# A graph attention layer on one core: four weight sums of the last head as DMA additions, with new orders for the last two heads

## The chip, the cores and the metric

The kernel runs on one core of one Trainium2 chip. The metric is the device time of one execution in microseconds (us). Engines are named as in the profile: PE is TensorE's matmul, PEld its weight load, DVE is VectorE, ACT is ScalarE, POOL is GpSimd, SP is SyncE, which here only issues DMAs. Each engine runs its own instructions strictly in the order in which they were written, and waits where an instruction needs the result of another engine or of a DMA.

## The reference

512 nodes with 768 features, 16,896 directed edges, eight attention heads in layer one and one in layer two; then a residual and a layer norm.

```python
def gat_layer(x, W, a_s, a_d, b, edge_index, concat):
    h = (x @ W).reshape(n, H, C)
    alpha_s = jnp.einsum('nhc,hc->nh', h, a_s)
    alpha_d = jnp.einsum('nhc,hc->nh', h, a_d)
    e = jax.nn.leaky_relu(alpha_s[src] + alpha_d[dst], NEG_SLOPE)
    m = jax.ops.segment_max(e, dst, num_segments=n)
    e = jnp.exp(e - m[dst])
    denom = jax.ops.segment_sum(e, dst, num_segments=n)
    alpha = e / (denom[dst] + EPS)
    out = jax.ops.segment_sum(h[src] * alpha[:, :, None], dst, num_segments=n)
    return out.reshape(n, H * C) + b          # here concat=True

h = gat_layer(x, W1, a_src1, a_dst1, b1, edge_list, concat=True)   # 8 heads of 768
h = jax.nn.elu(h)
out = gat_layer(h, W2, a_src2, a_dst2, b2, edge_list, concat=True) # W2: 6144 x 768
result = _layernorm(x + out, axis=-1)
```

## The kernel before

Edges are counted into a dense 512 x 512 matrix, so that each head is: a projection with W1 (512 x 768 by 768 x 768), a dense softmax over the logits, a product of the softmax with the projected features, an ELU, and a product with the head's 768 rows of W2, whose results are added up in the tile `h2` over all heads. After head 7 (the last) the second layer's softmax and its product with `h2` follow, then the layer norm and the output.

**Fewer products, more sums.** Each of these matrix products is done with fewer multiplications than the plain one. The softmax product of a head cuts both sides into 2 x 2 blocks and takes seven products, P1 to P7 (`mixed`, lines 960 to 1040; matmuls at L972). The W2 product cuts W2's 768 x 768 into 3 x 3 blocks of 256 x 256 and takes fifteen products, P0 to P14 (`second_thirds`, matmuls at L550; DVE empties a bank into `h2` at L558). Its left operands are sums of blocks of the ELU's output `gT` (`g_thirds`, DVE at L584 and L587). Its right operands are W2's blocks or sums of them, and these sums are made in two ways by `load_thirds`. Four of them are done while the block is loaded: SP loads one block, and POOL then issues a DMA that adds another block from HBM to it (`join`, L187). Eight more, called `w.P0`, `w.P1`, `w.P2`, `w.P3`, `w.P4`, `w.P6`, `w.P7`, `w.P10`, are additions of 128 x 512 elements by DVE (L200). `w.P0` adds block P12 to block P0, `w.P4` adds P13 to P4, `w.P1` and `w.P7` add P6 to P1 and P7; each writes over its own operand.

**Order.** Nothing is scheduled by the program itself. Strings of names fix the order in which the operations are written, and with it each engine's order: HEAD and SECOND for the heads, NEXT for the projection of the head after, END for head 7 and the whole second layer. HEAD's third string is used for head 6 alone. In these strings P10 to P72 are the seven softmax products for the three column chunks 0 to 2, `x`, `y`, `N`, `B`, `F` with a chunk's number are DVE's steps behind them (L990 for `x` and `y`, L1007, L1014, L1024), `b`, `f`, `n`, `nn`, `u`, `w` ACT's steps, `g.P..` the left sums, `m.P..` the W2 products, `e.P..` their emptying. `src`, `dst` (L420) and in END `ls`, `ld` (L1258) are row products of DVE for the logits; `rank`, `leak` (DVE) and `lift`, `out`/`part`, `in` (ACT) belong to the softmax; `l0` to `l3` and `r0` to `r3` are the sums of the next softmax product's operands.

**Around the change.** `loads` (one name in HEAD) issues all loads and joins of W2's rows of head 7 into the tiles `w2r` and `w2t`, during head 6. `vectors` loads the two vectors of the second layer's logits into `w1t` (L1192) at the end of head 6. Then x is loaded again by SP, and POOL adds the bias b2 to it by four DMAs of 384 KB (L1254). `rows0` and `rows1` (L1267) are the matmuls that make the second layer's logits; `spread` (L1289) and `own` (L1295) hand them on.

Of the kernel before, what the change touches and what calls it, by code (L numbers as in the profile page):

```python
# [37 lines left out]
def gat_pass(  # L38
# [119 lines left out]
    def load_thirds(slot, m, apart):  # L158

        def of(rows, k):  # L160
            return rows[k:k + HK + 1:HK] if apart else rows[2 * k:2 * k + 2]

        chunks = list(range(DC))

        def third(k, n):
# [16 lines left out]

        def load(o, k, n):
            return lambda: nc.sync.dma_start(o, part(k, n))

        def join(o, k, n):
            return lambda: nc.gpsimd.dma_start(o, part(k, n), accum_op=add)  # L187

        def row(k):
            return lambda: nc.sync.dma_start(rows_[:, k, :], m[k * P:(k + 1) * P, :])  # L190

        loads = {f"r{k}": row(k) for k in range(DC)}
        loads.update(P1=join(third(1, 1), 1, 2), P14=join(third(2, 1), 0, 1), p13=load(P13, 0, 2), P13=join(P13, 2, 2),
                     p12=load(P12, 0, 0), P12=join(P12, 1, 0), p11=load(P11, 0, 1), P11=join(P11, 1, 1))
        raw = {(k, n): third(k, n) for k in range(3) for n in range(3)}
        B_ = dict(P8=raw[0, 2], P9=raw[0, 0], P5=raw[0, 1], P13=P13, P12=P12, P14=raw[2, 1], P4=raw[2, 0], P0=raw[1, 2],
                  P3=raw[2, 2], P7=raw[1, 0], P1=raw[1, 1], P6=square(two, 0), P2=square(two, 1), P11=P11, P10=square(four, 1))

        def op(o, a, b, how):
            return lambda: nc.vector.tensor_tensor(B_[o], B_[a], B_[b], op=how)  # L200
# [552 lines left out]
    if not general:  # L753
# [85 lines left out]
    else:  # L839
# [252 lines left out]
    ops = softmax(q, 0)  # L1092
# [32 lines left out]
    def hold():  # L1125
# [25 lines left out]
        P61 P70 u1 w0 w.P6 x0 P71 P40 b0 vadd ls2 P30 w.P10 y0 w1 B0 P51 P62 w.P0 P41 u2 x1 w.P2 b1 P72 w2 ls3 w.P4 ld2 B1  # L1151
        P31 P42 f0 y1 P52 f1 F0 m.P2 x2 b2 ld1 F1 P32 B2 g.P9 g.P12 y2 m.P9 e.P2 w.P1 f2 m.P12 ld3 F2 g.P7 rows0 e.P9 g.P1
        w.P3 rows1 row2 e.P12 g.P13 m.P1 g.P6 g.P11 spread e.P1 m.P0 own m.P13 2lift1 w.P7 2lift2 2lift0 2leak1 g.P10 e.P0
        2rank1 m.P10 e.P13 2lift3 2leak0 2rank0 m.P4 2part1 e.P10 2leak2 2part0 2rank2 m.P11 e.P4 g.P8 2leak3 m.P6 seed g.P3
        m.P8 2rank3 g.P14 e.P6 2den0 2den2 2part2 2in1 m.P14 e.P11 e.P8 g.P5 e.P14 2den3 2part3 m.P3 2in2 m.P7 e.P3 2in0
        2den1 m.P5 e.P7 2in3 root c0 e.P5 f.P1.0 a0 f.P1.1 f.fork0 a2 a1 c1 f.P2.0 c2 f.fork1 y11.0 f.P6.0 sq0 xu0 a3 c3
        f.P5.0 f.P7.0 f.P6.1 xw0 f.P4.0 y22.0 xu1 sq2 y21.0 bn2 f.P3.0 f.P7.1 y12.0 bn4 f.P5.1 all2 all0 xw1 inv0 inv2 whole2
        f.P4.1 y22.1 sq3 whole0 f.P2.1 y21.1 bn3 all3 f.P3.1 y11.1 inv3 bn1 right3 left3 y12.1 bn5 all1 hint inv1 left1
        right1"""
# [305 lines left out]
```

## Time and profile before

| | |
|---|---|
| three runs | 614.26, 615.30 and 615.68 us; median 615.3 |
| the profiled execution's own time | 615.11 us |
| its span in the profile | 613.3 us |
| TensorE's granted clock | 0.997 |
| head 6, softmax product up to its first W2 product | about 492 to 511 us |
| head 6, W2 products | about 511 to 537 us |
| head 7, softmax product | about 537 to 559 us |
| head 7, W2 products | about 556 to 587 us |
| second layer's product, layer norm, output | about 587 to 613 us |

The span runs from the first to the last recorded instruction; the profiled execution took 1.8 us more than it. Times below are microseconds from the span's start. A row of the timeline gives the start, the length, the engine, the line, the operation, what is written from what with the shape, the number of merged instructions, and in brackets the idle time before it with what ended it. Instructions of DVE that follow each other overlap a little: one that lasts 0.68 us lets the next start after 0.60.

### The profile page before, as it was taken

The page shows a single profiled execution, that of the slowest core. Times are in us where ns is not written, and L with a number is a line of the kernel's source. Part 1 is how long each engine was busy: PE and PEld are TensorE (multiplying, and loading weights), DVE is VectorE, ACT ScalarE, POOL GpSimd, SP SyncE. Part 2 cuts the span into 40 slices and gives each one's busy share as a digit, 9 for nine tenths or more (in the row PEclk, how much of TensorE's full clock was granted, in tenths as well). Part 3 has the DMA queues.
Part 4 walks back from the last instruction along what each step waited for, and adds up shares of the span by engine and source line. Part 5 has one row for each costly group of instructions (what it writes and reads, how often), then busy time and mean ns, then how long its engine had stood idle before and what let it go on. Part 6 is the DMA issues. An engine that isn't in the chain of part 4 may idle for free.

```text
span 613.3 us, 8350 instructions
## 1 busy us (share of the span) xinstructions
PE 601.6 (98%) x2809; PEld 492.0 (80%) x2809; DVE 518.8 (85%) x1029; ACT 307.0 (50%) x570; POOL 94.2 (15%) x139
## 2 busy tenths in 40 slices
PE   8999999999999999999999999999999999999994
PEld 5665685788888888888888888888888888877862
DVE  7979968779997789778897789968896789889975
ACT  3128776624745176433736066442746056744753
POOL 1210103040301302021300303022300303020000
PEclk9999999999999999999999999999999999999998
DMA  8983898794947959394956949296965949282212
GB/s 284 324 175 81 246 266 211 210 293 80 345 68 247 198 192 228 57 342 74 335 95 205 238 132 281 45 322 108 311 126 157 265 108 241 41 234 39 45 25 107
DMA packets 96399, 113.19 MB, mean 185 GB/s; under 512 B 42918, under 2 KB 77406, under 8 KB 95454
## 3 DMA queue, kind: packets, MB, share of 16 engines
q1 hardware_dynamic: 75374, 89.26, 46.1%
q0 software_dynamic: 20544, 22.75, 23.5%
q10 hardware_dynamic: 432, 0.59, 0.3%
q8 instruction: 24, 0.39, 0.2%
q14 instruction: 25, 0.20, 0.1%
HBM read 99.05 MB, written 2.90 MB: 166 GB/s over the span
## 4 chain that ended last, share of the span: by engine, by line
PE 91%; DVE 5%; DMA 3%; issue 1%; ACT 0%; SPq 0%; DVEq 0%; ACTq 0%
PE mm L550 23%; PE mm L470 18%; PE mm L972 14%; PE mm L411 11%; PE tr L470 4%; PE bc L470 4%; PE tr L972 3%; PE bc L972 3%; PE tr L550 3%; PE bc L550 3%; PE mm L1331 2%; DMA hs<-in_x_dram 2%; PE bc L781 1%; DVE scr L1258 1%; DMA w1t<-in_L_gnn_a_dst_dram 1%; PE mm L658 1%
## 5 line engine op out<-in xcount | busy, mean ns | idle before, releaser
L558 DVE TENSOR_TENSOR h<-h,mm 128x512 f32<-128x512 f32 x80 | 54.5, 681 | 9.3 <-PE mm L550 8.6
L476 ACT ACTIVATE hs<-mm 128x512 f32<-128x512 f32 x26 | 15.5, 598 | 80.6 <-PE mm L470 79.9
L187 POOL DMA_DIRECT2D w2t<-in_L_gnn_W_dram x21 | 28.3, 1665 | 165.7 <-DVE h L558 56.2
L478 DVE TENSOR_TENSOR hs<-hs,mm 128x512 f32<-128x512 f32 x38 | 26.1, 687 | 27.0 <-PE mm L470 19.9
L972 PE MATMUL mm<-PT,hs 128*128 128x256 f32 x196 | 47.8, 380 | 0.7 <-DVE gT L1007 0.7
L550 PE MATMUL mm<-w1r,gT 128*128 128x256 f32 x192 | 44.1, 379 | 0.0
L901 ACT ACTIVATE q<-q,rden 128x512 f32<-128x512 f32 x28 | 20.2, 720 | 46.1 <-DVE rden L885 45.8
L972 PEld LDWEIGHTS mm<-PT,hs 128*128 128x128 f32 x196 | 36.8, 190 | 6.4 <-ACT u L983 1.3
L909 ACT COPY PT<-zr 128x1024 uint16<-128x1024 uint16 x35 | 40.3, 1158 | 1.9 <-DMA zr<-pS 1.8
L550 PEld LDWEIGHTS mm<-w1r,gT 128*128 128x128 f32 x192 | 36.4, 190 | 5.1 <-DVE h L558 0.2
L187 POOL DMA_DIRECT2D w2r<-in_L_gnn_W_dram x14 | 18.3, 1310 | 140.6 <-DVE gT L1024 57.7
L698 ACT ACTIVATE q<-q,nmax 128x512 f32<-128x512 f32 x36 | 26.0, 723 | 25.3 <-DVE nmax L695 25.3
L470 PE MATMUL mm<-w2r,gT 128*128 128x256 f32 x144 | 33.7, 379 | 0.0
L420 DVE SCALAR_TENSOR_TENSOR scr<-hs,a_s 128x768 bf16<-128x768 f32 x32 | 30.6, 955 | 0.7
L420 DVE SCALAR_TENSOR_TENSOR scr<-hs,a_d 128x768 bf16<-128x768 f32 x32 | 30.4, 951 | 0.3
L470 PEld LDWEIGHTS mm<-w2r,gT 128*128 128x128 f32 x144 | 27.4, 190 | 3.7
L550 PE MATMUL mm<-w1t,gS 128*128 128x256 f32 x128 | 30.2, 379 | 0.0
L470 PE MATMUL mm<-w2r,xT 128*128 128x256 f32 x128 | 29.9, 379 | 0.0
L972 PE MATMUL mm<-pS,gS 128*128 128x256 f32 x120 | 29.3, 379 | 0.0
L904 ACT COPY pS<-q 128x1024 uint16<-128x1024 uint16 x27 | 28.1, 1044 | 0.7
L550 PEld LDWEIGHTS mm<-w1t,gS 128*128 128x128 f32 x128 | 24.3, 190 | 3.3
L470 PEld LDWEIGHTS mm<-w2r,xT 128*128 128x128 f32 x128 | 24.3, 190 | 3.3
(375 smaller groups left out, 1483.3 us busy)
## 6 DMA issues: line engine op xcount, KB each, us to landing
w2r<-in_L_gnn_W_dram SPq DMA_DIRECT2D x48, 384.0 KB
w1r<-in_L_gnn_W_dram SPq DMA_DIRECT2D x43, 384.0 KB
gT<-xd SPq DMA_DIRECT2D x6, 1280.0 KB
w2t<-in_L_gnn_W_dram SPq DMA_DIRECT2D x21, 256.0 KB
w2t<-in_L_gnn_W_dram POOLq DMA_DIRECT2D x21, 256.0 KB, 9.5
w1t<-in_L_gnn_W_dram SPq DMA_DIRECT2D x18, 256.0 KB
w1t<-in_L_gnn_W_dram POOLq DMA_DIRECT2D x18, 256.0 KB, 5.4
w2r<-in_L_gnn_W_dram POOLq DMA_DIRECT2D x14, 256.0 KB, 8.7
```

Of the source, the lines that this page charges most:

```text
L187: return lambda: nc.gpsimd.dma_start(o, part(k, n), accum_op=add)
L411: nc.tensor.matmul(ps[:, :HALF], A_[p][:, k, i * P:(i + 1) * P], B_[p][:, k, :], start=start and k == 0, stop=k == HK - 1, skip_group_chec ...
L420: return [lambda al=al, a=a, sign=sign: nc.vector.scalar_tensor_tensor(scr, HS[h][:, t, :], sign, a, op0=ALU.mult, op1=ALU.mult, accum_out ...
L470: nc.tensor.matmul(bank[chain][:, i * TH:(i + 1) * TH], A_[p][:, k, i * P:(i + 1) * P], B_[p][:, k, :], start=first and i == k == 0, stop= ...
L478: nc.vector.tensor_tensor(out(o), out(o), ps, op=how)
L550: nc.tensor.matmul(bank[chain][:, i * TH:(i + 1) * TH], A_[p][:, k, i * P:(i + 1) * P], B_[p][:, k, :], start=first and i == k == 0, stop= ...
L558: nc.vector.tensor_tensor(out(o), out(o), ps, op=how)
L698: nc.scalar.activation(q, q, AF.Exp, bias=nmax, scale=-1.0, accum_out=dens[t])
L901: nc.scalar.activation(q, q, AF.Copy, scale=rden)
L904: nc.scalar.copy(apart.rearrange("p (h n) -> p h n", h=2), q.bitcast(U16).rearrange("p (n h) -> p h n", h=2))
L909: copy(PT.rearrange("p s n -> p (s n)").bitcast(U16).rearrange("p (s n h) -> p s n h", s=NT, h=2)[:, :, t * P:(t + 1) * P, :], parted.pop( ...
L972: nc.tensor.matmul(st[bank][:, :HN], A_[p][:, k, c * P:(c + 1) * P], B_[p][:, k, :], start=start and k == 0, stop=k == 1, skip_group_check ...
```

## The change

Four of the eight sums of W2's rows of head 7 are no longer DVE additions. A second set of operations, `qP0`, `qP4`, `qP1` and `qP7`, does the same additions as DMAs from SBUF to SBUF, issued by POOL, with the DMA's own addition. `qP0` is issued at the end of `loads`; the other three stand in END right behind `w.P10`. The heads before use DVE as they did. The strings for head 6 (HEAD) and for head 7 (END) are written anew.

```diff
+        def onto(o, a):
+            return lambda: nc.gpsimd.dma_start(B_[o], B_[a], accum_op=add)
         return B_, loads, dict(
             P6=op("P6", "P14", "P4", ALU.subtract), P4=op("P4", "P13", "P4", add), P2=op("P2", "P12", "P13", ALU.subtract),
             P10=op("P10", "P5", "P1", add), P0=op("P0", "P12", "P0", add), P1=op("P1", "P6", "P1", add),
-            P3=op("P3", "P10", "P3", ALU.subtract), P7=op("P7", "P6", "P7", add))
+            P3=op("P3", "P10", "P3", ALU.subtract), P7=op("P7", "P6", "P7", add),
+            **{f"q{o}": onto(o, a) for o, a in (("P0", "P12"), ("P4", "P13"), ("P1", "P6"), ("P7", "P6"))})
...
-    END = """P10 in2 P11 fork0 in3 P20 r0 fork1 P21 n0 nn0 r1 P12 n1 ld0 P50 fork2 N0 r3 nn1 r2 P22 N1 n2 ls0 nn2 N2 P60 u0 ls1
...
+    END = """P10 P11 in2 fork0 in3 P20 r0 fork1 P21 n0 nn0 r1 n1 P12 ld0 P50 fork2 N0 r3 nn1 r2 P22 N1 n2 ls0 nn2 N2 P60 u0 ls1
+        P61 P70 u1 w0 w.P6 x0 P71 P40 b0 vadd ls2 P30 w.P10 q.P1 q.P4 q.P7 ld1 y0 w1 B0 P51 P62 P41 u2 x1 w.P2 b1 P72 w2 ls3
...
             for n in "r1 r4 P1 r2 r5 P14 r0 r3 p13 P13 p12 P12 p11 P11".split():
                 loads2[n]()
+            W_["qP0"]()
...
-    ops.update({f"w.{p}": f for p, f in W_.items()})
+    ops.update({f"w.{p}": W_[p] for p in ("P6", "P10", "P2", "P3")})
+    ops.update({f"q.{p}": W_[f"q{p}"] for p in ("P4", "P1", "P7")})
```

What moves on the engines is shown at three places. PE's order is the same as before, but for the numbers of two PSUM banks; SP's order is the same.

**POOL, from the joins of head 7 to the end.** Before (`w2r`, `w2t` hold W2's rows of head 7, `hs` is x with the bias):

```order
L187 DMA w2r<-in_L_gnn_W_dram 128x2x256 x2
L187 DMA w2t_306<-in_L_gnn_W_dram 128x2x256 x2
L187 DMA w2t_318<-in_L_gnn_W_dram 128x2x256
L1254 DMA hs<-in_L_gnn_b_dram 128x768 x4
L1369 MEMSET st 128x2
L1370 MEMSET st 128x1
```

and with the change (L1258 is the former L1254):

```order
L187 DMA w2r<-in_L_gnn_W_dram 128x2x256 x2
L187 DMA w2t_306<-in_L_gnn_W_dram 128x2x256 x2
L187 DMA w2t_318<-in_L_gnn_W_dram 128x2x256
L203 DMA w2r<-w2t_306 128x2x256
L1258 DMA hs<-in_L_gnn_b_dram 128x768 x4
L1374 MEMSET st 128x2
L1375 MEMSET st 128x1
...
L203 DMA w2r<-w2t_317 128x2x256
L203 DMA w2r<-w2t_306 128x2x256
L203 DMA w2r<-w2t_317 128x2x256
```

The first L203 is `qP0`, between the joins and the bias; the last three are `q.P1`, `q.P4` and `q.P7`, at the very end of POOL's work.

**DVE in head 6, between the end of the logits and the third chunk.** Before (L200 is a weight sum, L990 `x` and `y`, L690 and L695 the softmax's `leak` and `rank`, L584 and L587 left sums; `zr<-bc,twice,w` is `x2`):

```order
L1007 SCALAR_TENSOR_TENSOR gT<-nl,zl 128x256
L990 SCALAR_TENSOR_TENSOR zr<-mm_96,both,u 128x256
L1014 SCALAR_TENSOR_TENSOR gT<-w,mm_98 128x256
L690 SCALAR_TENSOR_TENSOR q<-q 128x512
L695 ISA q,nmax<-q,cnt 128x512
L695 ISA nmax 128x1
L1024 SCALAR_TENSOR_TENSOR gT<-nr,zr 128x2x256
L584 TENSOR_TENSOR u_632<-gT 128x512
L587 SCALAR_TENSOR_TENSOR gS<-gT 128x512
L690 SCALAR_TENSOR_TENSOR q<-q 128x512
L990 SCALAR_TENSOR_TENSOR zr<-bc,twice,w 128x256
```

and with the change:

```order
L1011 SCALAR_TENSOR_TENSOR gT<-nl,zl 128x256
L200 TENSOR_TENSOR w1r<-w1t_118,w1r 128x2x256
L994 SCALAR_TENSOR_TENSOR zr<-mm_96,both,u 128x256
L694 SCALAR_TENSOR_TENSOR q<-q 128x512
L699 ISA q,nmax<-q,cnt 128x512
L699 ISA nmax 128x1
L1028 SCALAR_TENSOR_TENSOR gT<-nr,zr 128x2x256
L1018 SCALAR_TENSOR_TENSOR gT<-w,mm_98 128x256
L591 SCALAR_TENSOR_TENSOR gS<-gT 128x512
L588 TENSOR_TENSOR u_632<-gT 128x512
L694 SCALAR_TENSOR_TENSOR q<-q 128x512
L994 SCALAR_TENSOR_TENSOR zr<-bc,twice,w 128x256
```

`w.P4` of head 6 stands here now, ahead of `y1`, and `B1` (L1014, now L1018) stands behind `F1` instead of ahead of `leak0`. Earlier in the same head, `w.P2` moved from ahead of the transposition for the logits to behind `y0`, `w.P6` to ahead of `N0`; later, `l0` moved to right behind `x2`.

**DVE in head 7, up to the first left sum.** Before (L1258 are the row products `ls` and `ld`; `w2r<-w2t` are weight sums in place; `u_632<-gT` is the left sum `g.P9`):

```order
L990 SCALAR_TENSOR_TENSOR zr<-mm_96,both,u 128x256
L1014 SCALAR_TENSOR_TENSOR gT<-w,mm_95 128x256
L200 TENSOR_TENSOR w2r<-w2t_306,w2r 128x2x256
L990 SCALAR_TENSOR_TENSOR zr<-mm_97,twice,w 128x256
L200 TENSOR_TENSOR w2t_317<-w2t_306 128x512
L1258 SCALAR_TENSOR_TENSOR scr,al_245<-h_631,w1t_118 128x768
L200 TENSOR_TENSOR w2r<-w2t_306,w2r 128x2x256
...
L1258 SCALAR_TENSOR_TENSOR scr,al_245<-h_631,w1t_252 128x768
L1024 SCALAR_TENSOR_TENSOR gT<-nr,zr 128x2x256
L1014 SCALAR_TENSOR_TENSOR gT<-w,tr 128x256
L584 TENSOR_TENSOR u_632<-gT 128x512
```

and with the change:

```order
L1262 SCALAR_TENSOR_TENSOR scr,al_245<-h_631,w1t_252 128x768
L994 SCALAR_TENSOR_TENSOR zr<-mm_96,both,u 128x256
L1018 SCALAR_TENSOR_TENSOR gT<-w,mm_95 128x256
L994 SCALAR_TENSOR_TENSOR zr<-mm_97,twice,w 128x256
L200 TENSOR_TENSOR w2t_317<-w2t_306 128x512
L1262 SCALAR_TENSOR_TENSOR scr,al_245<-h_631,w1t_118 128x768
...
L994 SCALAR_TENSOR_TENSOR zr<-bc,twice,w 128x256
L1028 SCALAR_TENSOR_TENSOR gT<-nr,zr 128x2x256
L588 TENSOR_TENSOR u_632<-gT 128x512
L1018 SCALAR_TENSOR_TENSOR gT<-w,tr 128x256
```

The two sums into `w2r` (`w.P0`, `w.P4`) are gone ahead of `g.P9`, the row product `ld1` stands earlier, and `B2` (L1014, now L1018) behind `g.P9`. Behind this place `w.P1` and `w.P7` are gone as well, and in the softmax of the second layer `rank` of tiles 2 and 3 stands later among the left sums.

More of the change, by code (lines that the diff above doesn't have):

```diff
@@ L1135, in gat_pass @@
         P42 g.P7 e.P2 b2 m.P9 P32 lift2 w.P4 B2 e.P9 y2 f2 buffers g.P1""",
-        """P10 P50 w.P10 src0 fork0 P60 u0 src1 P20 n0 P70 w.P2 w0 row loads x0 nn0 N0 w.P0 P11 P40 fork1 P30 b0 y0 f0 dst0 P51
-        w.P6 F0 B0 P61 u1 P21 n1 dst1 P71 w1 x1 nn1 w.P1 N1 P12 fork2 P41 lift0 b1 P31 y1 f1 B1 leak0 P52 P62 u2 rank0 F1
-        lift1 g.P9 g.P12 P22 P72 leak1 n2 w2 m.P2 x2 nn2 P32 rank1 N2 w.P4 g.P7 P42 e.P2 y2 m.P9 b2 B2 f2 l0 g.P1 e.P9 out0"""]
+        """P10 P50 w.P10 src0 fork0 P60 u0 src1 P20 n0 P70 w0 row loads x0 nn0 w.P6 N0 w.P0 P11 P40 fork1 P30 b0 y0 f0 w.P2 dst0
+        P51 F0 B0 P61 u1 P21 n1 dst1 P71 w1 x1 nn1 w.P1 N1 P12 fork2 w.P4 P41 lift0 b1 P31 y1 f1 leak0 P52 P62 u2 rank0 F1 B1
+        lift1 g.P12 P22 g.P9 P72 leak1 n2 w2 m.P2 x2 nn2 l0 P32 rank1 N2 g.P7 P42 e.P2 y2 m.P9 b2 B2 f2 e.P9 g.P1 out0"""]
     SECOND = ["""m.k1 m.P2.0 F2 m.P2.1 g.0 g.1 lift3 e.P2.1 leak1 m.P6.0 m.u0 e.P2.0 m.P6.1 buffers g.2 rank1 m.P7.0 g.3 m.u1 m.w0
@@ L1149, in gat_pass @@
         vectors l1 e.P3 m.P7 m.P5 e.P7 l2 l3 e.P5 e.P8"""]
-    END = """P10 in2 P11 fork0 in3 P20 r0 fork1 P21 n0 nn0 r1 P12 n1 ld0 P50 fork2 N0 r3 nn1 r2 P22 N1 n2 ls0 nn2 N2 P60 u0 ls1
[L1151 to L1159, printed above, removed]
+    END = """P10 P11 in2 fork0 in3 P20 r0 fork1 P21 n0 nn0 r1 n1 P12 ld0 P50 fork2 N0 r3 nn1 r2 P22 N1 n2 ls0 nn2 N2 P60 u0 ls1
+        P61 P70 u1 w0 w.P6 x0 P71 P40 b0 vadd ls2 P30 w.P10 q.P1 q.P4 q.P7 ld1 y0 w1 B0 P51 P62 P41 u2 x1 w.P2 b1 P72 w2 ls3
+        ld2 P31 P42 f0 y1 B1 P52 f1 F0 m.P2 x2 b2 F1 g.P9 P32 B2 g.P12 y2 m.P9 e.P2 f2 m.P12 ld3 F2 g.P7 rows0 e.P9 g.P1 w.P3
+        rows1 row2 e.P12 g.P13 m.P1 g.P6 g.P11 spread e.P1 m.P0 own m.P13 2lift1 2lift2 2lift0 2leak1 g.P10 e.P0 2rank1 e.P13
+        2lift3 2leak0 2rank0 m.P10 m.P4 2part1 e.P10 2leak2 2part0 g.P8 m.P11 e.P4 2rank2 2leak3 m.P6 seed g.P3 m.P8 g.P14
+        e.P6 2den0 2den2 2part2 2in1 m.P14 2rank3 e.P11 e.P8 g.P5 e.P14 2den3 2part3 m.P3 2in2 m.P7 2in0 2den1 e.P3 m.P5 e.P7
+        2in3 root c0 a0 e.P5 f.P1.0 f.P1.1 f.fork0 a2 a1 c1 f.P2.0 c2 f.fork1 y11.0 f.P6.0 sq0 xu0 a3 c3 f.P5.0 f.P7.0 f.P6.1
+        xw0 f.P4.0 y22.0 xu1 y21.0 sq2 bn2 f.P3.0 f.P7.1 y12.0 bn4 all2 f.P5.1 all0 xw1 inv0 inv2 whole2 f.P4.1 y22.1 sq3
+        whole0 f.P2.1 y21.1 bn3 all3 f.P3.1 y11.1 inv3 bn1 right3 left3 y12.1 bn5 all1 hint inv1 left1 right1"""
@@ L1246, in gat_pass @@
             run(NEXT[min(h, 1)], ops)
-            assert all(n.startswith(("w.", "in0", "weigh", "part", "turn")) for n in ops), sorted(ops)
+            assert all(n.startswith(("w.", "T.q", "in0", "weigh", "part", "turn")) for n in ops), sorted(ops)
             kept = {n: f for n, f in ops.items() if n.startswith("w.")}
```

## The prediction, as it was made before the result

> **What bounds the kernel now.** I read the page's busy shares, then the chain of waits, then windows of 20 us, because a share over 613 us hides where the slack lies.
>
> ```profile
> span 613.3 us, 8350 instructions
> PE 601.6 (98%) x2809; PEld 492.0 (80%) x2809; DVE 518.8 (85%) x1029; ACT 307.0 (50%) x570; POOL 94.2 (15%) x139
> PE 91%; DVE 5%; DMA 3%; issue 1%; ACT 0%; SPq 0%; DVEq 0%; ACTq 0%
> 500.00:520.00 20.00, 19.58 (x91) 16.66 (x90) 18.68 (x39) 14.89 (x31) 6.08 (x5) 1.00 0.97 237
> 540.00:560.00 20.00, 18.41 (x84) 15.21 (x83) 17.78 (x40) 10.43 (x26) 3.75 (x10) 1.00 0.69 176
> 560.00:580.00 20.00, 19.88 (x109) 15.86 (x108) 19.77 (x39) 10.20 (x19) 0.00 (x0) 1.00 0.14 26
> 580.00:600.00 20.00, 20.00 (x75) 13.82 (x74) 16.16 (x34) 10.66 (x19) 0.00 (x0) 1.00 0.16 27
> ```
>
> PE sets the pace. The windows (columns: length, then busy us of PE, PEld, DVE, ACT, POOL, the clock, DMA share, GB/s) show where PE waits in the stages that the change touches: 0.42 us in 500 to 520, 1.59 us in 540 to 560, 0.12 us in 560 to 580. Only that can be won. PE's rows name the places:
>
> ```profile
> 508.75 1.89 PE L550 MATMUL mm<-w1t,gT 128*128 128x256 f32 x8
> 511.06 1.13 PE L972 MATMUL bc<-PT,gS 128*128 128x256 f32 x4 [0.42 <-DVE zr L990]
> 543.33 1.89 PE L972 MATMUL mm<-pS,xS 128*128 128x256 f32 x8
> 545.94 1.99 PE L972 MATMUL mm<-PT,hs 128*128 128x256 f32 x8 [0.72 <-DVE gT L1007]
> 547.77 1.03 PE L972 MATMUL mm<-pS,hs 128*128 128x256 f32 x4
> 549.06 1.13 PE L972 MATMUL mm<-PT,xS 128*128 128x256 f32 x4 [0.27 <-DVE zr L990]
> 557.80 1.03 PE L972 MATMUL bc<-PT,xS 128*128 128x256 f32 x4
> 559.43 1.99 PE L550 MATMUL mm<-w2r,u 128*128 128x256 f32 x8 [0.60 <-DVE u L584]
> 561.26 1.89 PE L550 MATMUL mm<-w2t,gS 128*128 128x256 f32 x8
> 564.90 1.99 PE L550 MATMUL mm<-w2r,gS 128*128 128x256 f32 x8
> 566.74 1.02 PE L1289 MATMUL mm<-nr,picks 128*128 128x512 f32 x2
> ```
>
> A wait costs more than the bracket says. Eight matmuls that follow on without a wait take 1.73 us from start to start, four 0.865 (half); behind a wait they take 0.10 more (559.43 to 561.26 is 1.83). So m.P9 should have begun at 557.80 + 0.865 = 558.67 and began at 559.43: **0.77 + 0.10 = 0.87 us**. P32 at 511.06 should have begun at 510.48: 0.58 + 0.10 = 0.68 us. P70 at 545.94 (due 545.06) lost 0.98, P30 at 549.06 (due 548.63) 0.53.
>
> The two middle ones don't come from the weight sums. DVE stands still for a load that SP issues behind head 6's softmax:
>
> ```profile
> 543.08 0.96 DVE L1258 SCALAR_TENSOR_TENSOR scr<-h,w1t 128x768 bf16<-128x768 f32 x1 [2.19 <-DMA w1t<-in_L_gnn_a_dst_dram]
> 537.13 0.34 SPq L1192 DMA_DIRECT2D w1t<-in_L_gnn_a_dst_dram  x1
> ```
>
> The order of DVE, ACT and SP between this load and `w.P10` is unchanged, so those 1.51 us stay, only moved along with PE.
>
> **Part 1: head 6.** P32 must wait for `x2`, which waits on DVE:
>
> ```profile
> 505.47 0.48 DVE L990 SCALAR_TENSOR_TENSOR zr<-mm,both,u 128x256 f32<-128x256 f32 x1 [0.77 <-PE mm L972]
> 506.32 0.42 DVE L1014 SCALAR_TENSOR_TENSOR gT<-w,mm 128x256 f32<-128x256 f32 x1 [0.36 <-ACT w L1011]
> 506.83 0.63 ACT L1021 ACTIVATE nr<-nr 128x512 f32<-128x512 f32 x1
> 507.37 0.69 DVE L695 CUSTOM_DVE_ANT_0 q<-q,cnt 128x512 f32<-128x512 f32 x1
> 509.92 0.68 DVE L690 SCALAR_TENSOR_TENSOR q<-q 128x512 f32<-128x512 f32 x1
> 510.52 0.48 DVE L990 SCALAR_TENSOR_TENSOR zr<-bc,twice,w 128x256 f32<-128x256 f32 x1
> 511.86 0.68 DVE L200 TENSOR_TENSOR w1r<-w1t,w1r 128x512 f32<-128x512 f32 x1
> ```
>
> `w.P4` (511.86) moves into the idle 0.77 us ahead of `y1`, which PE and not DVE times, so it costs nothing there; without that gap it would cost 0.60. `B1`'s wait of 0.36 for ACT goes, because `leak0` and `rank0` run first (505.87 to 507.18). Then `F1` waits for ACT's second pass until 507.46 and runs to 508.08; `B1` 0.33, two left sums 1.20 and `leak1` 0.60 follow, so `x2` starts at 510.21 instead of 510.52: **0.31 us** won of the 0.68. Lower bound: nothing, if ACT's chain (`lift1`, the copy `w2`) isn't earlier too; upper: 0.68. I take 0.31. `l0` (0.87) now stands behind `x2`, and `rank1` is later by 0.56; it only delays ACT's exponent, and DVE catches up by 516, since `w.P4` and `l0` are no longer in its way there. `vectors` and the load of a_dst go behind ACT's last copy of head 6, which PE times, and so move along.
>
> **Part 2: head 7.** Four sums leave DVE:
>
> ```profile
> L200 DVE TENSOR_TENSOR w2r<-w2t,w2r x5: 680/680/682, 551.2 to 568.5; 128x512 f32<-128x512 f32 x5
> 549.88 0.68 DVE L200 TENSOR_TENSOR w2t<-w2r 128x512 f32<-128x512 f32 x1
> 550.48 0.47 DVE L990 SCALAR_TENSOR_TENSOR zr<-mm,both,u 128x256 f32<-128x256 f32 x1
> 556.00 0.63 ACT L1020 ACTIVATE nr<-zr 128x512 f32<-128x512 f32 x1 [0.75 <-DVE zr L990]
> 558.36 0.41 DVE L1014 SCALAR_TENSOR_TENSOR gT<-w,tr 128x256 f32<-128x256 f32 x1
> 558.69 0.68 DVE L584 TENSOR_TENSOR u<-gT 128x512 f32<-128x512 f32 x1
> ```
>
> The row of five (count, shortest, median and longest duration in ns, first and last start) holds the four and `w.P3`, which stays. Each takes 0.60 (549.88 to 550.48), so 2.40 us of DVE in all, but only what stands ahead of a PE wait counts. Ahead of `g.P9` (558.69) are `w.P0` and `w.P4`, 1.20, and `B2`'s 0.33, which moves behind: 557.16. `ld1` only moves within. `F1` ahead of it now waits for ACT: `y1` ends near 555.3, ACT's two passes take 1.29 (630 ns twice, and the step between), `F1` runs 556.62 to 557.22, and `g.P9` is done at 557.90. PE is due at 558.67, so the 0.87 goes, with 0.77 to spare. Next on DVE: `B2`, `g.P12` (558.83; due 560.39), `y2`, `ld3`, `F2` (561.31; the logit rows due 562.12), `g.P7`, `e.P9`, `g.P1` (563.11; m.P1 due 563.9). All are in time, so the remaining 0.12 at m.P1 (564.90) and its 0.10 go too: **0.22 us**. Bounds for this part: 0 and 1.09; I take 1.09, since every margin is positive.
>
> **The DMA additions** must land before PE reads them: m.P1 near 563.9, m.P0 567, m.P4 572, m.P7 582 (all on the old clock). The trace has no addition of this size from SBUF; the nearest rows:
>
> ```profile
> 512.34 3.68 POOL L187 DMA_DIRECT2D w2t<-in_L_gnn_W_dram  x3 [1.53 <-DMA w2t<-in_L_gnn_W_dram]
> w2t<-in_L_gnn_W_dram POOLq DMA_DIRECT2D x6, 256.0 KB, 8.0
> w2t<-w2t POOLq DMA_DIRECT2D x2, 576.0 KB, 6.0
> 544.52 3.73 POOL L1254 DMA_DIRECT2D hs<-in_L_gnn_b_dram  x4 [28.50 <-PE mm L972]
> DMA to landing us min/median/max: 4.7/8.1/9.8
> 554.00:556.00 2.00, 2.00 (x11) 1.77 (x10) 2.00 (x6) 1.22 (x3) 0.00 (x0) 1.00 0.49 86
> ```
>
> `qP0` waits in POOL's queue for P12's join (last join 516, 8 us to landing, so 524 at worst) and holds up only the bias, which starts at 544.5: nothing lost. `q.P1` waits for `w.P10`, that is until 550.56; POOL is through with the bias at 548.25. Its bytes queue behind the bias additions (1.5 MB, landing 4.7 to 9.8 us after issue; the DMA share falls to 0.49 in 554 to 556). Low bound 550.56 + 4.7 = 555.3; high bound, the slowest bias landing, 557.2, plus 6.0 for an addition over twice as large, 563.2. I take 559, and some 2 us more for each of the two behind it. Even the high bound is ahead of 563.9. Price in the sum: 0.
>
> The rule that speaks against this is in the Trainium skill, SBUF — State Buffer, section "SBUF: two separate sides": POOL writes the descriptors of its DMAs itself, and is locked out while DVE runs an instruction in a two-port mode, such as a float32 copy. In the rows above POOL took 1.2 us per issue while DVE was busy throughout with float32 two-operand instructions, so the trace shows no lock for these, and DVE's new order holds no such copy between 550 and 566.
>
> **Sum.** 0.31 + 0.87 + 0.22 = 1.40 us off the profiled execution's 615.11, so 613.71. That execution lies 0.2 below the median of 615.3; against the median: **613.9**.
> From 568 on PE had no wait, and I find none new. `rank` of tile 3 goes behind left sums and an emptying, but ACT's copy of tile 2 no longer stands behind it, and the last copies into `PT` decide:
>
> ```profile
> 583.98 3.30 ACT L909 COPY PT<-zr 128x1024 uint16<-128x1024 uint16 x3 [0.96 <-DMA zr<-pS]
> ```
>
> They ended at 587.28. With tile 2's copy first and tile 3's exponent near 579.3, I have them end near 586.2 on the old clock, some 1.1 us earlier, which is what PE itself has gained by then. That is enough, but nothing is left over.
>
> **Rivals.**
> *Only one of the two places gives way.* For it: `x2` also hangs on ACT's `lift1` and copies, and the copies into `PT` gain just what PE gains; each microsecond of lateness there is lost. Against: in head 7 all margins are over half a microsecond. If the tail loses 0.7 us or the head 7 part is halved, 614.6; if nothing is won, 615.3.
> *The additions are late.* If an addition from SBUF with 1 KB pieces is as slow as the slowest bias addition (9.8) and can't begin before that has landed (557.2), `q.P1` lands at 567.0; m.P1 waits 3.1 us and PE everything behind it: 613.9 + 3.1 = 617.0. The break-even is a landing at 565.3, 14.7 us behind the issue. For it: 16 DMA engines are full until 554. Against: the joins, of the same size and piece, landed in 8.0 beside loads, and nothing else moves after 556.
> *POOL can't issue while DVE is busy.* DVE pauses 0.23 us in all of 560 to 580; if `q.P1` is issued only at 568, it lands at 573 (4.7 more), m.P1 waits 9 us: 623. Against: POOL's three issues in 3.68 us from 512.34, with DVE busy. The skill's page above names such a lock.
>
> **Chances.** As summed: 0.56. One place only, or nothing won: 0.26. Additions late: 0.14; POOL held off or another new wait: 0.04. What a measurement of this kernel can tell from no change is about 0.2%, 1.2 us; 614.1 is that line. The first case lies just beyond it, the second within, the last two are slower: faster 0.56, same 0.26, slower 0.18. The likeliest case's own range is 613.3 to 614.4 (bounds of part 1, and 0.3 for the tail). For 8 in 10 the range runs up through the second case and the mildest of the late ones: 613.1 to 616.0.
>
> **What would show it.** Right: P32's bracket near 0.1 instead of 0.42; no bracket at m.P9 and m.P1; the waits at P70 and P30 still there, near 1.0 us together; the L203 additions landing 5 to 12 us after issue; PE without waits from 566 on. Wrong: a wait of PE for a DMA into `w2r` at m.P1, or for `PT` or `xT` after 586; a longer wait of DVE for a_dst; or DVE's row products pushed so that `y1` and the sums behind it come later.

## The result and the profile after

The changed kernel takes 613.22 us (median of 13 runs, 613.0 to 614.16), the kernel before 614.84 us in the 13 runs beside it (614.01 to 615.68): a ratio of 0.9976, 95% interval 0.9968 to 0.9985. That is 1.6 us less, where 1.40 was forecast, and inside the range of 613.1 to 616.0. The forecast time itself was 613.9; 0.5 of the 0.7 us between the two is the kernel before, whose 13 runs have a lower median than the three runs (615.3) that the forecast started from.

The page of the changed kernel (span; busy time and share of each engine; the chain of waits by engine):

```profile
span 611.2 us, 8354 instructions
PE 601.0 (98%) x2809; PEld 492.7 (81%) x2809; DVE 517.0 (85%) x1025; ACT 307.2 (50%) x570; POOL 99.0 (16%) x143
PE 96%; DVE 2%; DMA 1%; issue 0%; ACT 0%; DVEq 0%
```

Its windows of 20 us (length, then busy us of PE, PEld, DVE, ACT, POOL, clock, DMA share, GB/s):

```profile
500.00:520.00 20.00, 20.00 (x93) 17.29 (x93) 19.47 (x41) 14.56 (x31) 7.29 (x6) 1.00 1.04 245
540.00:560.00 20.00, 19.14 (x88) 16.19 (x87) 17.92 (x40) 10.91 (x26) 7.44 (x13) 1.00 0.92 205
560.00:580.00 20.00, 20.00 (x110) 16.07 (x109) 18.47 (x39) 11.54 (x20) 0.00 (x0) 1.00 0.21 40
```

PE has no idle time left in 500 to 520 and 560 to 580; in 540 to 560 it still idles 0.86 us. Its timeline at the places of the prediction (start, us, then in brackets the idle time ahead and what ended it):

```profile
508.45 1.89 PE L554 MATMUL mm<-w1t,gT 128*128 128x256 f32 x8
510.32 1.13 PE L976 MATMUL bc<-PT,gS 128*128 128x256 f32 x4
544.84 1.99 PE L976 MATMUL mm<-PT,hs 128*128 128x256 f32 x8 [0.58 <-DVE gT L1011]
547.97 1.13 PE L976 MATMUL mm<-PT,xS 128*128 128x256 f32 x4 [0.27 <-DVE zr L994]
557.57 1.89 PE L554 MATMUL mm<-w2r,u 128*128 128x256 f32 x8
562.74 1.99 PE L554 MATMUL mm<-w2r,gS 128*128 128x256 f32 x8
601.63 1.45 PE L1336 MATMUL mm<-h,pS 128*128 128x384 f32 x4
```

The brackets at P32 (510.32), m.P9 (557.57) and m.P1 (562.74) are gone; those at P70 (544.84) and P30 (547.97) are still there. The rest of the timeline that the prediction spoke of: DVE's wait for a_dst, the three additions on POOL, `g.P9`, and the last copy into `PT`:

```profile
541.98 0.96 DVE L1262 SCALAR_TENSOR_TENSOR scr<-h,w1t 128x768 bf16<-128x768 f32 x1 [2.05 <-DMA w1t<-in_L_gnn_a_dst_dram]
549.77 3.68 POOL L203 DMA_DIRECT2D w2r<-w2t  x3 [2.42 <-DVE w2t L200]
556.43 0.69 DVE L588 TENSOR_TENSOR u<-gT 128x512 f32<-128x512 f32 x1
583.66 1.16 ACT L913 COPY PT<-zr 128x1024 uint16<-128x1024 uint16 x1 [0.99 <-DMA zr<-nr]
```

**How the profiles are compared.** The two spans differ by 2.1 us, more than the medians. Part of that has nothing to do with the change: PE reached head 6's m.P2 (the `w1t,gT` row) at 508.75 before and at 508.45 after, and 0.28 of these 0.30 us are there already at the first row of head 6's softmax product (492.32 against 492.04), behind code that is the same in both. So I count from that row. Its start is taken off the starts of P70, m.P9, m.P1 and of the last four matmuls, which gives the length of each stretch. After: 544.84 - 508.45 = 36.39, 557.57 - 544.84 = 12.73, and so on. All kernels that follow are read in this way:

| kernel | m.P2 to P70 | P70 to m.P9 | m.P9 to m.P1 | m.P1 to the last | in all | median us | ratio to before, 95% interval |
|---|---|---|---|---|---|---|---|
| before | 37.19 | 13.49 | 5.47 | 38.90 | 95.05 | 614.84 | 1 |
| changed | 36.39 | 12.73 | 5.17 | 38.89 | 93.18 | 613.22 | 0.9976 (0.9968 to 0.9985) |
| head 6's order alone | 37.38 | 13.49 | 5.48 | 38.89 | 95.24 | 614.86 | 0.9999 (0.9990 to 1.0008) |
| changed, head 6's old order | 36.73 | 12.74 | 5.16 | 38.89 | 93.52 | 614.03 | 0.9987 (0.9978 to 0.9997) |
| both orders, sums on DVE | 37.03 | 13.41 | 5.81 | 38.89 | 95.14 | 615.10 | 1.0002 (0.9992 to 1.0011) |
| DMA sums, both old orders | 36.60 | 13.30 | 5.27 | 39.70 | 94.87 | 615.00 | 1.0000 (0.9991 to 1.0009) |
| changed, ld0 later | 35.65 | 12.34 | 5.17 | 38.89 | 92.05 | 611.61 | 0.9950 (0.9936 to 0.9963) |
| the same again | 35.65 | 12.42 | 5.16 | 38.90 | 92.13 | 611.92 | 0.9958 (0.9945 to 0.9970) |
| before, ld0 later | 36.04 | 12.85 | 5.48 | 38.89 | 93.26 | 613.25 | 0.9973 (0.9964 to 0.9982) |
| both orders, sums on DVE, ld0 later | 35.65 | 12.77 | 5.81 | 38.89 | 93.12 | 613.43 | 0.9977 (0.9967 to 0.9988) |
| DMA sums, old orders, ld0 later | 36.01 | 12.79 | 5.27 | 38.90 | 92.97 | 613.17 | 0.9974 (0.9964 to 0.9984) |
| changed, head 6's old order, ld0 later | 36.14 | 12.51 | 5.17 | 38.89 | 92.71 | 612.28 | 0.9944 (0.9931 to 0.9958) |
| changed, additions issued late | 36.91 | 12.73 | 6.99 | 38.86 | 95.49 | 614.26 | 0.9990 (0.9981 to 1.0000) |

The stretches come from one execution each, the medians from 5 to 13 runs. The runs of the kernel before were shared within a group of experiments and had medians of 614.95, 614.96, 614.85 and 615.29 us, so across groups the ratio is the fairer column.

### The profile page after: what moved, and what is told of

Same layout as the page of the kernel before. It is cut to its first block, busy times and chain, and to the rows that moved or that the text cites. A ratio compares the mean times of both kernels' runs of the same rounds, so it can differ in the third digit from the quotient of the medians.

```text
span 611.2 us, 8354 instructions
## 1 busy us (share of the span) xinstructions
PE 601.0 (98%) x2809; PEld 492.7 (81%) x2809; DVE 517.0 (85%) x1025; ACT 307.2 (50%) x570; POOL 99.0 (16%) x143
## 4 chain that ended last, share of the span: by engine, by line
PE 96%; DVE 2%; DMA 1%; issue 0%; ACT 0%; DVEq 0%
PE mm L554 24%; PE mm L474 18%; PE mm L976 15%; PE mm L415 12%; PE bc L474 4%; PE tr L474 4%; PE tr L976 4%; PE bc L976 3%; PE tr L554 3%; PE bc L554 3%; PE mm L1336 2%; PE mm L662 1%; PE bc L785 1%; DMA w1t<-in_L_gnn_a_dst_dram 1%; PE tr L415 1%; PE bc L271 1%
```

## The experiments

### The parts of the change, one at a time

**Head 6's order alone** (kernel before, with the new string for head 6):

```diff
-        """P10 P50 w.P10 src0 fork0 P60 u0 src1 P20 n0 P70 w.P2 w0 row loads x0 nn0 N0 w.P0 P11 P40 fork1 P30 b0 y0 f0 dst0 P51
...
+        """P10 P50 w.P10 src0 fork0 P60 u0 src1 P20 n0 P70 w0 row loads x0 nn0 w.P6 N0 w.P0 P11 P40 fork1 P30 b0 y0 f0 w.P2 dst0
...
```

> The kernel before with nothing but the new order of head 6 (no DMA additions, head 7 as before). Theory: x2 starts 0.3 to 0.45 us earlier and P32 waits for it only 0.14 us and not 0.58; everything behind moves by 0.3 to 0.45 us, so 614.4 to 614.5 us against 614.8. The waits at P70 and P30 (1.51 us), at m.P9 (0.87) and at m.P1 (0.22) stay. Rival: the 0.74 us by which PE was ahead at P32 in the two profiles is all this order, and 0.2 more behind it: 613.9. Second rival: what is won at P32 is taken up by a longer wait of DVE for a_dst: 614.8.

614.86 us, no change. The timeline of this kernel (SP's issue of the load, DVE's and PE's waits):

```profile
536.30 0.34 SPq L1192 DMA_DIRECT2D w1t<-in_L_gnn_a_dst_dram  x1
543.09 0.96 DVE L1258 SCALAR_TENSOR_TENSOR scr<-h,w1t 128x768 bf16<-128x768 f32 x1 [3.03 <-DMA w1t<-in_L_gnn_a_dst_dram]
545.95 1.99 PE L972 MATMUL mm<-PT,hs 128*128 128x256 f32 x8 [1.57 <-DVE gT L1007]
```

P32 no longer waits, and SP issues the load of a_dst 0.83 us earlier than in the profile before (536.30 against 537.13). But it lands 6.79 us behind its issue instead of 5.95, DVE starts at the same 543.09, and P70 at the same 545.95. In this execution the second rival holds: what head 6 won is waited away at P70.

**Head 7 alone** (the changed kernel, with the old string for head 6; the diff is the one above, the other way round).

> The changed kernel with the old order of head 6: the four sums by DMA and the new order of head 7 alone. Theory: the waits at m.P9 (0.87) and m.P1 (0.22) are gone, the one at P32 is back (0.68), P70 and P30 as in the changed kernel: 1.1 us off, 613.7 us. Rival (head 7 only pays because head 6 came earlier): 614.3 or more.

614.03 us, halfway between the theory's 613.7 and the rival's 614.3, so the time doesn't decide. The timeline does: PE's only brackets from head 6 on are those at P70 (0.62) and P30 (0.28), so m.P9 and m.P1 are in time, as the theory has it. The stretches from P70 to m.P9 and on to m.P1 are those of the changed kernel (12.74 and 5.16).

**Both orders, the sums on DVE:**

```diff
-            W_["qP0"]()
...
-    ops.update({f"w.{p}": W_[p] for p in ("P6", "P10", "P2", "P3")})
-    ops.update({f"q.{p}": W_[f"q{p}"] for p in ("P4", "P1", "P7")})
+    ops.update({f"w.{p}": W_[p] for p in ("P6", "P10", "P2", "P3", "P0", "P4", "P1", "P7")})
```

and in END `q.P1 q.P4 q.P7` out, `w.P0` behind `P62`, `w.P4` behind `ls3`, `w.P1` behind `e.P2`, `w.P7` behind `2lift1`.

> The changed kernel with both new orders, but the four sums on DVE again (P0 and P4 ahead of g.P9, P1 ahead of g.P1, P7 behind own), no DMA additions. Theory (the 1.2 us of DVE ahead of g.P9 are what counted there): g.P9, done 557.04 in the changed kernel, comes 1.2 us later than that, 0.7 behind the 557.57 at which PE is due; with the restart 0.8 us are lost, and up to 0.6 more at m.P1: 614.0 to 614.6 us. Rival (the order did it, and the sums cost nothing where they were): 613.2 us and no bracket at m.P9.

615.10 us: the order alone wins nothing, and the time is above what the theory gave. PE still waits at m.P9:

```profile
559.00 1.99 PE L554 MATMUL mm<-w2r,u 128*128 128x256 f32 x8 [0.32 <-DVE u L588]
```

The table shows what the order did: the stretch to m.P9 is 0.08 shorter, the one from m.P9 to m.P1 0.34 longer. As I read it, `B2`'s 0.33 moved from ahead of `g.P9` to behind it, and from there stands ahead of `F2` and `g.P1`, which PE's next products need; no run has `B2` moved by itself.

**The DMA additions alone, in the old orders:**

```diff
-        P61 P70 u1 w0 w.P6 x0 P71 P40 b0 vadd ls2 P30 w.P10 y0 w1 B0 P51 P62 w.P0 P41 u2 x1 w.P2 b1 P72 w2 ls3 w.P4 ld2 B1
+        P61 P70 u1 w0 w.P6 x0 P71 P40 b0 vadd ls2 P30 w.P10 q.P1 q.P4 q.P7 y0 w1 B0 P51 P62 P41 u2 x1 w.P2 b1 P72 w2 ls3 ld2 B1
```

and `w.P1` and `w.P7` out further on.

> The kernel before, orders of heads 6 and 7 as they were, with only the four sums swapped for DMA additions (issued behind w.P10). Theory: DVE has 1.2 us less ahead of g.P9 and 1.8 less ahead of g.P1, so m.P9 and m.P1 don't wait, although B2 still stands ahead of g.P9 (0.33 of a margin of 0.5 to 0.8): 613.7 us, the same as the run with the new order of head 7. Rival (the deal of head 7 is needed too): m.P9 still waits, 614.2 us.

615.00 us: nothing won either, and both numbers were missed. PE's timeline and DVE's:

```profile
558.29 1.99 PE L554 MATMUL mm<-w2r,u 128*128 128x256 f32 x8 [0.40 <-DVE u L588]
586.01 1.56 PE L1337 MATMUL tr<-h,PT 128*128 128x384 f32 x4 [0.17 <-ACT PT L913]
```

```profile
554.34 0.69 DVE L1028 SCALAR_TENSOR_TENSOR gT<-nr,zr 128x512 f32<-128x512 f32 x1 [0.25 <-ACT nr L1025]
555.34 0.48 DVE L994 SCALAR_TENSOR_TENSOR zr<-bc,twice,w 128x256 f32<-128x256 f32 x1 [0.30 <-PE bc L976]
555.74 0.95 DVE L1263 SCALAR_TENSOR_TENSOR scr<-h,w1t 128x768 bf16<-128x768 f32 x1
556.61 0.69 DVE L1028 SCALAR_TENSOR_TENSOR gT<-nr,zr 128x512 f32<-128x512 f32 x1
```

Of the DVE time that the sums left free, 0.55 us is idle, ahead of things that wait for ACT and PE. Then the row product `ld1` (555.74, 0.87 to the next start) stands between `x2` and `g.P9` as before. At the end the copies into `PT` are late: the stretch from m.P1 on is 0.81 longer. This is not the order's doing. The copies wait for a transposition by DMA (`zr`), and the run with the same order further down (ld0 later) has no such loss. SP's issue of this DMA and ACT's copy, here and there:

```profile
579.21 1.23 SPq L910 DMA_TRANSPOSE zr<-pS  x1
583.73 3.30 ACT L913 COPY PT<-zr 128x1024 uint16<-128x1024 uint16 x3 [2.04 <-DMA zr<-pS]
```

```profile
578.14 1.66 SPq L910 DMA_TRANSPOSE zr<-pS  x1
581.18 2.22 ACT L913 COPY PT<-zr 128x1024 uint16<-128x1024 uint16 x2 [0.57 <-DMA zr<-pS]
```

From issue to copy it is 4.52 us here and 3.04 there (3.43 in the kernel before).

### The wait for a_dst

The load of a_dst lay ahead of every wait in head 7. From SP's issue to DVE's start it took 5.95 us before, 5.80 in the changed kernel, and in the four experiments above 6.79, 5.85, 6.44 and 5.78, by no rule that goes with the change. Two more kernels further down (additions issued late, extra copies) are the same as the changed kernel up to this place, and there it took 6.32 and 5.92. PE pays for it: in all eight profiles the bracket at P70 is 1.46 or 1.47 us shorter than DVE's wait for this load. So I moved DVE's first product with a_dst behind four other DVE instructions, in the changed kernel and in the kernel before (a part of END's first line):

```diff
-P12 ld0 P50 fork2 N0 r3 nn1 r2 P22 N1 n2
+P12 P50 fork2 N0 r3 nn1 r2 P22 N1 ld0 n2
```

> The changed kernel with one DVE instruction moved: the first row product with a_dst (ld0) four DVE instructions later (behind N1), so that DVE has work while the load of a_dst is on its way. Theory now (the landing of a_dst, 5.8 to 6.8 us behind its issue in six profiles, sets DVE's start in head 7, and by it the waits at P70 and P30 and, in the kernel before, those at m.P9 and m.P1): DVE no longer waits for a_dst, P70 and P30 don't wait, 1.2 to 1.4 us less than the changed kernel: 611.9 us, and the runs lie closer together than the 1.2 us of the changed kernel. Rival (N0 and the attention sums behind it wait for ACT or PE anyway, so that DVE idles there all the same): 613.2 us.

> The kernel before with the same single move (ld0 behind N1): sums on DVE, old orders. Theory now: DVE has no idle between the landing of a_dst and g.P9 in the kernel before, so the 2.2 us that it idles ahead of the landing are the source of all the waits of head 7; with 1.5 us or more of them filled, the waits at P70 (0.98), P30 (0.53), m.P9 (0.87) and m.P1 (0.22) all go or nearly: 612.3 to 612.9 us, below the changed kernel without any DMA addition. Rival (the prediction's own reading: the weight sums ahead of g.P9 are a load of their own): P70 and P30 go, m.P9 and m.P1 still wait since PE is earlier by as much: 613.4 us or more.

The changed kernel falls to 611.61 us (612 in a second group, below), and its windows are full:

```profile
540.00:560.00 20.00, 20.00 (x93) 17.07 (x91) 19.25 (x42) 11.19 (x27) 7.43 (x13) 1.00 0.93 209
560.00:580.00 20.00, 20.00 (x110) 16.20 (x109) 18.38 (x42) 12.08 (x20) 0.00 (x0) 1.00 0.30 39
```

DVE's timeline there has 0.35 and 0.16 of idle in place of 2.05:

```profile
540.48 0.43 DVE L1011 SCALAR_TENSOR_TENSOR gT<-nl,zl 128x256 f32<-128x256 f32 x1 [0.35 <-ACT nl L1008]
542.79 0.96 DVE L1262 SCALAR_TENSOR_TENSOR scr<-h,w1t 128x768 bf16<-128x768 f32 x1 [0.16 <-DMA w1t<-in_L_gnn_a_dst_dram]
```

That the runs would lie closer together isn't shown: the two groups of five span 0.7 and 1.0 us, the changed kernel's thirteen 1.2.

In the kernel before the same move gives 613.25 us, as much as the whole change. My theory there fell: PE's timeline still has the wait at m.P9, as the rival said,

```profile
556.90 1.99 PE L550 MATMUL mm<-w2r,u 128*128 128x256 f32 x8 [0.57 <-DVE u L584]
```

0.57 instead of 0.60. DVE has no idle time between its wait near 540 and m.P9 in either kernel, so m.P9 hangs on the sum of DVE's work. Filling 1.83 of the 2.19 us of idle brought m.P9 1.79 us nearer to m.P2 (50.68 to 48.89; 0.26 of it comes from P32, where this execution lost less), and PE, freed at P70 and P30, stood there earlier as well. The time lies between the theory's 612.9 and the rival's 613.4, nearer to the rival. The weight sums are a load of their own.

### What the additions are worth without that wait

> The changed kernel with ld0 behind N1 once more, to have more runs of it beside the two below: 611.6 us (611.3 to 612.0), no wait of PE for DVE from head 6 on.

> Both new orders and ld0 behind N1, but the four sums on DVE and no DMA addition. Theory (DVE wins some 2.3 us by the move and PE 1.7, so that m.P9's wait of 0.32 in the run with the sums on DVE shrinks but 1.2 us of sums still stand ahead of g.P9): m.P9 waits 0 to 0.3 us, up to 0.2 at m.P1: 611.7 to 612.2 us. Rival (the additions by DMA are worth their full 1.1 us also without the wait for a_dst): 612.7 us. Second rival (once a_dst is out of the way the sums cost nothing): 611.6 us and no wait.

> The old orders of heads 6 and 7 with the four sums by DMA, and ld0 behind N1. Theory (in the old order the 1.2 us taken off DVE turn into idle time ahead of x2, since ld1, 0.88, and B2, 0.33, stay between x2 and g.P9): m.P9 still waits 0.2 to 0.5 us and the copies into PT are late by some 0.3 at the end: 612.7 to 613.2 us, no better than the kernel before with the same move (613.25). Rival (the sums are what counts and the order isn't): 611.8 us.

With the sums on DVE in both new orders 613.43 us, with the additions in the old orders 613.17, with both 611.92 beside them (one of the eleven runs of the old orders took 2,259 us; without it their median is 613.08). PE's row at m.P9, with the sums on DVE and with the additions in the old orders, each from its own timeline:

```profile
558.37 1.99 PE L554 MATMUL mm<-w2r,u 128*128 128x256 f32 x8 [0.32 <-DVE u L588]
```

```profile
557.21 1.99 PE L554 MATMUL mm<-w2r,u 128*128 128x256 f32 x8 [0.40 <-DVE u L588]
```

The waits are 0.32 and 0.40, exactly as with ld0 in its old place. My forecast that the move would shrink the first fell, and of the three the rival that gives the additions their full worth is the nearest: in the stretches it is 12.77 - 12.34 = 0.43 and 5.81 - 5.17 = 0.64, together 1.07 us. The medians lie 1.5 apart, so the time is above this rival's 612.7 as well. The theory for the old orders held in its time and in the wait at m.P9; the late copies at the end, which it also had, didn't come (38.90 from m.P1 on).

**Head 6's order without the wait for a_dst:**

> The changed kernel's head 7 (four sums by DMA, new order) with ld0 behind N1, and the old order of head 6: what head 6's order is worth when a_dst no longer takes it back. Theory (in the profiles the old order costs PE 0.07 to 0.44 us at P32, by how early the row q is read back, and 0.2 more between 516 and 524): 0.3 to 0.4 us more than with both orders, 612.0 to 612.3 us. Rival (the new order of head 6 is worth the 0.8 us that lie between the medians of the changed kernel and of the run without it): 612.5 us. Second rival (it is worth nothing): 611.6 to 611.9 us.

612.28 us. The stretches say 0.6 us more than with both orders (92.71 against 92.05 and 92.13), of which 0.27 is at P32,

```profile
510.60 1.13 PE L976 MATMUL bc<-PT,gS 128*128 128x256 f32 x4 [0.25 <-DVE zr L994]
```

and 0.22 by 523. The ratios (0.9944 against 0.9950 and 0.9958) can't tell the kernels apart. What head 6's order is worth stays open: nothing in its own experiment, 0.8 us between the changed kernel and the run without it, 0.4 to 0.7 between the medians here.

### The price of the additions

**Behind the bias additions.** The landings of the three additions behind `w.P10`, in the changed kernel and in the second group of the same with ld0 later:

```profile
DMA to landing us min/median/max: 5.9/6.4/7.6
```

```profile
DMA to landing us min/median/max: 9.6/10.1/10.7
```

With ld0 later POOL issues them 4.6 us behind its first bias addition (548.69 against 544.11) and not 6.4 (549.77 against 543.39), and they take 7.5 to 10.7 us in the four profiles with ld0 later that have them, against 5.6 to 7.8 in the four with ld0 in its old place and the additions issued early. So they can be as slow as the 9.8 of the prediction's rival. They are in time all the same, since in the slowest case the first is in place by 548.69 + 10.7 = 559.4 and m.P1 begins at 561.66.

**Issued late** (`w.P10` and the three additions behind `e.P2` in place of ahead of `ld1`; parts of two lines of END):

```diff
-P30 w.P10 q.P1 q.P4 q.P7 ld1 y0
+P30 ld1 y0
...
-m.P9 e.P2 f2 m.P12 ld3
+m.P9 e.P2 w.P10 q.P1 q.P4 q.P7 f2 m.P12 ld3
```

> The changed kernel with w.P10 and the three DMA additions behind it moved from ahead of ld1 to behind e.P2: they are issued some 9 us later, at 559, with no other bytes on the way; m.P1 needs q.P1 at 562.7. Theory (an addition of 256 KB lands 3.9 us behind its issue where nothing else moves, as the first of the four did): landing near 563.0, m.P1 waits 0.2 to 0.4 us, 613.4 to 613.7 us. With the 6.4 us that the three took beside the bias additions: landing 565.5, m.P1 waits 2.7 us, 616.0. Rival of the prediction (as slow as the slowest bias addition, 9.8): landing 568.9, a wait of 6.2 us, 619.4.

614.26 us, 1.0 above the changed kernel. From the timeline of this kernel and, for the landings, its view by line of the additions:

```profile
559.78 3.68 POOL L203 DMA_DIRECT2D w2r<-w2t  x3 [12.45 <-DVE w2t L200]
564.53 1.97 PE L554 MATMUL mm<-w2r,gS 128*128 128x256 f32 x8 [1.75 <-DVE h L562]
```

```profile
DMA to landing us min/median/max: 4.7/4.8/5.8
```

The bracket names DVE's `h`, but if the first addition is the one that took 4.7 it lands at 559.78 + 4.7 = 564.5, just where m.P1 starts. That lies between the two estimates (3.9 and 6.4), so neither forecast time was met, and far from the rival's 9.8. In this profile the stretch from m.P9 to m.P1 is 1.82 us longer, in the medians the kernel loses 1.0; that a late addition makes m.P1 wait, as the prediction had it, is shown, its price in the medians only roughly.

**DVE copies beside POOL's issues** (one execution; `p10` is a 128x512 piece of `w2t`; the first two lines are parts of a line of END):

```diff
-w.P10 q.P1 q.P4 q.P7 ld1 y0
+w.P10 q.P1 q.P4 q.P7 cp0 cp1 cp2 cp3 cp4 cp5 cp6 cp7 ld1 y0
...
+    ops.update({f"cp{j}": lambda: nc.vector.tensor_copy(p10, p10) for j in range(8)})
```

> The changed kernel with eight extra float32 copies 128x512 on DVE (a tile onto itself) right behind w.P10, so that they run while POOL issues the three additions. Rival of the prediction (POOL is held off while DVE runs float32 copies): the row of the three issues, 3.68 us in the changed kernel, grows by about the time of the copies (2.5 to 4.5 us) or starts behind them. Theory (POOL issues beside them): 3.68 to 3.8 us, starting 0.4 us behind the end of w.P10. The time itself is longer in both, by the 2.5 to 4.5 us of DVE that stand ahead of y0.

619.69 us. The view by tile of `w2t` (count, then shortest, median and longest duration in ns, first and last start):

```profile
L1270 DVE COPY w2t<-w2t x8: 426/428/887, 550.4 to 554.4; 128x512 f32<-128x512 f32 x8
L203 POOL DMA_DIRECT2D w2r<-w2t x3: 1207/1637/2182, 550.7 to 552.3; - x3
```

The copies ran from 550.45 to 554.79, over all three issues. POOL's issues took 3.73 us (3.68 in the changed kernel), so POOL wasn't held off. It was DVE that was held: the fourth and fifth copy took 651 and 887 ns instead of 428, beside POOL's second and third issue. The 4.34 us of copies then stood ahead of `y0`, and PE waited 3.94 us. The stretch from P70 to m.P9 grew by more than this wait, by 5.89 us (18.62 against 12.73): behind the wait PE's granted clock was lower (the column behind POOL's busy time):

```profile
554.00:556.00 2.00, 0.00 (x0) 0.00 (x0) 1.97 (x6) 0.00 (x0) 0.44 (x1) 1.00 1.21 194
556.00:558.00 2.00, 1.42 (x4) 1.22 (x5) 2.00 (x5) 1.17 (x3) 0.00 (x0) 0.73 1.20 183
558.00:560.00 2.00, 2.00 (x6) 1.56 (x6) 1.22 (x4) 1.53 (x3) 0.00 (x0) 0.50 0.14 21
```

## Why the prediction was right, point by point

**Part 2, the waits at m.P9 and m.P1 (0.87 and 0.22): right in mechanism and nearly in size.** The stretches give 13.49 - 12.73 = 0.76 and 5.47 - 5.17 = 0.30, together 1.06 for 1.09. Forecast was `g.P9` done 0.77 us ahead of PE; it came 0.45 ahead (557.12, with PE at 557.57). One sentence in it said too little: "`ld1` only moves within". Without the new order of head 7, in which `ld1` comes earlier and `B2` later, the four sums buy next to nothing, as the additions in the old orders show: 0.19 at m.P9 and 0.20 at m.P1. Nor does the order buy anything without the additions. The prediction took the sums' 1.20 and `B2`'s 0.33 off in one step and priced neither alone. How much of the order's part is `ld1` and how much `B2` no run separates.

**Part 1, P32 (0.31): the number came near by luck.** P32 comes 0.44 earlier behind m.P2 than before (510.32 - 508.45 = 1.87 against 2.31). But the cause that the prediction read off, `B1` behind ACT, has another cause behind it in ACT's timeline of the kernel before, which the prediction did not follow back:

```profile
504.84 0.72 ACT L686 ACTIVATE q<-q,al_d 128x512 f32<-128x512 f32 x1 [0.57 <-DMA q<-drow]
```

ACT waited for a row that SP reads back from HBM. In the other profiles with the old order that wait is at most 0.38, and P32 starts 1.88 to 2.14 behind m.P2 instead of 2.31. With the new order it is 1.86 or 1.87 in all eight profiles. So 0.44 is what this one execution lost; the other profiles with the old order, one of them of the same code up to here (the kernel before with ld0 later), lose 0.01 to 0.27. The due time was off as well: 1.73 behind m.P2 was asked for, and 1.87 is what remains without any wait.

**"Those 1.51 us stay, only moved along with PE": the step that failed.** In the changed kernel the waits at P70 and P30 were 0.58 and 0.27, near enough to the forecast. But the load's landing doesn't move along with PE: it varies by 1.0 us over the eight profiles, by 0.5 over the three whose code is the same up to there (5.80, 5.92 and 6.32), and PE pays the difference at P70. In its profile that took back all that head 6's order won, and it may be one reason why a single profile and the medians differ by some tenths of a microsecond. And most of the 1.51 us could be had by moving one instruction (1.13 in the stretches, 1.6 in the medians): the forecast looked for what the change does, and took this wait as given.

**The price of the additions, 0: right.** They landed 5.9 to 7.6 us behind their issue (estimate 8.4, bounds 4.7 and 12.6). The first was in place by 557.4 at the latest, 5 us ahead of m.P1. The rival of late additions was right about how slow they can be (9.6 to 10.7 us in one profile with ld0 later), but not about when: it let these 9.8 us begin at 557.2 and land at 567.0, and the slowest first addition was in place by 559.4. POOL wasn't held off, neither in the changed kernel nor beside the extra copies.

**The tail, "nothing is left over": right.** The last copy into `PT` ended at 584.82, 2.46 us earlier than before, while PE came 2.17 earlier. That it needed the new order isn't shown: with the additions in the old orders the stretch from m.P1 on is 39.70 in one profile and 38.90 in the other, and the difference is one landing of a DMA.

## What to carry to other kernels

Follow a wait back to its first cause before you price it: where it ends on a DMA landing, the number on the page is one draw, and what is won ahead of it may be waited away behind it. Taking work off an engine may pay only if what is left on it is dealt out so that the freed time lies ahead of the instruction that is waited for; here neither the additions in the old orders nor the new orders without the additions won anything measurable, and the two together won 0.24%. Ahead of a load that lands late, first look for work that can be put in front of its first reader: one DVE instruction moved was worth as much as the whole change, and together they give 0.4 to 0.5%.

## What the runs showed of the hardware

- The same load of 384 KB, issued in the same place of SP's order, took 5.78 to 6.79 us from issue to its reader's start in eight profiles. A transposition by DMA at the end took 3.04 us in one profile and 4.52 in another, with the same order.
- An addition of 256 KB from SBUF to SBUF landed 4.7 to 5.8 us behind its issue in a row of three with nothing else on the way, and 5.6 to 10.7 behind the bias additions, more the sooner it was issued behind them. `qP0`, one addition beside the end of other loads, landed 3.9 us behind its issue in the changed kernel and 4.1 to 6.6 in the eight other profiles that have it.
- Beside POOL's issues, DVE's float32 copies were held and POOL's issues were not (two of eight took 651 and 887 ns instead of 428; 3.73 against 3.68 us). The Trainium skill, SBUF — State Buffer, section "SBUF: two separate sides", says that such a copy and POOL's writing of descriptors exclude each other and that whoever comes first holds the ports. The trace agrees that they can collide, and here the cost fell on DVE; most of the copies beside the three issues weren't held.
- Behind PE's wait of 3.94 us its granted clock was 0.73 and 0.50 in the next windows of 2 us; behind the wait of 1.75 us in the run with late additions it stayed at 1.00.
- The unchanged start of the kernel varies too: head 6's m.P2 began between 507.9 and 509.95 us in the profiles, and the latest of them had PE wait 1.3 us for the first load of x.
